# Rows stored in parts, loads split between stores, weights one item later: a change to an attention and convolution kernel

## The chip, the cores and the metric

The kernel runs on one core of a Trainium2 chip. The time is in microseconds of device time for one execution. A core has five engines that run their own instruction lists beside each other: PE (matrix products), DVE (elementwise work on vectors), ACT (functions and copies), POOL and SP (here both used only to start transfers; DVE and ACT also do the arithmetic that PE does not). Transfers are carried by the core's 16 DMA engines. SP and ACT start them by hardware queues, POOL by a software queue.

## The reference

Two images of 256 channels and 64 × 64 points pass through two layers. In plain code, with all that only reshapes left out:

```python
# layer 0
q, k, v = heads(Wq x + bq) / sqrt(32), heads(Wk x + bk), heads(Wv x + bv)   # 8 heads, 4096 points
fuse = softmax(q k^T) v
h = Wf [x, fuse] + bf
x = h * m + x * (1 - m)                        # m: the mask, resized to 64 x 64
# layer 1
x = x * sigmoid(relu(x ca_w1 + ca_b1) ca_w2 + ca_b2)       # per point, over channels
x = x + (window attention over 8 x 8 windows, 4 heads) out_w + out_b
x = channel shuffle of x in 4 groups
y = relu(bn1(conv 7x7 of x, 64 groups, 4 channels in, 1 out))
y = bn2(conv 7x7 of y, 64 groups, 1 channel in, 4 out)
out = x * sigmoid(y)
```

Everything is in 32-bit floats.

## The kernel before

**Projections (0 to 175 us).** q, k and v are computed for 16 chunks of 512 columns (2 images × 8) and stored to DRAM. v is copied out of PSUM by ACT into a staging tile with tag "v" (L499 to L511) and stored by POOL; the last chunk is copied in two halves, by ACT and by DVE. The staging pool has two places, so a tile waits for the stores of the one two before. Then a flag that DVE computed decides a branch; here the first of two arms runs.

**Attention (175 to 2685 us).** `pipeline` runs over 1024 slots: image b, chunk c of 512 query columns, head group g of 4 heads, key block m of 128 keys. Each slot has 16 score matmuls (L666), four exponentials on ACT (L679), products (L718) and a running sum of the exponentials on DVE (L724). When a chunk is through, `denominators` (L752, tile dn) sums over the keys by matmuls, and DVE divides (f, L785). `at(delay, action)` puts an action off by so many slots: a chunk's `stage(b, c)` begins DN + 8 + late slots after the chunk's last one; late is 5, but 0 for the last two chunks, (1,6) and (1,7). The stage is a generator: `run_stages` takes it one step further at every fourth slot, so that its matmuls (hy: fuse convolution; ca1, ca2: channel attention; qk: projection; sc: window scores; pt, o: transposes and products; op: out-projection) lie between the attention's. It makes u (L861), projects q and k of the windows (`project`), and ends with storing the chunk's rows xo to x_s in DRAM (L1047). The stage of (1,6) spans the last chunk's slots; the stage of (1,7) runs when there are none left.

**Convolutions.** `convolve` is a generator over 26 items. Item k is a set u of 4 of the 64 groups, for one image or for both: k = 0 to 8 are u = 0 to 8 of image 0; k = 9 to 15 are u = 2 to 8 of image 1; k = 16 to 21 are u = 9 to 14 of both images at once ("pairs"); k = 22 to 25 are single again (u = 15 of each image, then u = 1 and u = 0 of image 1). The loop at k does, in this order:

- `conv1(k+1)`: the first convolution on PE. Single items have 56 matmuls (L1177); pairs (`conv1_pairs`, L1144) use two operands that DVE made: dx, differences of neighbouring points (L1116), and both, sums of neighbouring weights (L1121, tile "both", "botha" in the profile). At its end it makes them for item k+2 (`differences(k+2)`).
- `conv2(k)`: the second convolution on PE (L1203), then tanh and a copy on ACT (L1214, L1220) into z. z has four places.
- `gate(k)`: z times x on DVE (L1230).
- loads of rows: SP brings the rows of a later item from x_s (L1095), one transfer for each image, up to item k+6.
- `store(k)`: 12 stores for each image, 3 blocks of rows × 4 (L1257; L1255 where ACT starts them), dealt out to the queues of POOL, SP and, in the last two items, ACT.
- `load_w`: SP brings the weights of one u, 896 KB (L1088), into a tile of tag "e", which has 8 places. While `weights[0] <= 1 + EB` (EB is 8) one set is loaded in every item; the later ones, from w10 on, one in every item from k = EARLY + 4 = 13 (EARLY is 9).

Each engine works through its list in the order of the program. The framework counts SP's and ACT's transfers over 8 counters in turn, so that a transfer waits until the one eight before is done.

```python
                z = conv2(k)
...
                gate(k, z)
...
                store(k, z)
                if weights and (weights[0] <= 1 + EB or k >= EARLY + 4):
                    load_w(weights.popleft())
```

Of the kernel before, what the change touches and what calls it, by code (L numbers as in the profile page):

```python
# [57 lines left out]
def conv_seq_kernel(ctx: ExitStack, tc: tile.TileContext, a, out):  # L58
# [315 lines left out]
    with (  # L374
# [109 lines left out]
        for i, (b, c) in enumerate(chunks):  # L484
# [14 lines left out]
            for copy, ms in evict:  # L499
                v = st0.tile([P, KC, 4, P], F32, tag="v", name=f"vst_{b}_{c}_{ms.start}")  # L500
                copy(  # L501
                    v[:, :, ms].rearrange("p g m d -> p m g d"),
                    sv[:, ms].rearrange("p m (g d) -> p m g d", g=KC),
                )
                for g in range(KC):
                    nc.gpsimd.dma_start(
                        v_s[b, g, c][:, ms.start * P : ms.stop * P],
                        v[:, g, ms].rearrange("p m d -> p (m d)"),
                    )
# [46 lines left out]
    def pipeline(arm, shifted, pools):  # L556
# [232 lines left out]
        def stage(b, c):  # L789
# [71 lines left out]
            nc.vector.scalar_tensor_tensor(u, t, 1.0, x1, ALU.add, ALU.mult)  # L861
# [4 lines left out]
            def project(hc):  # L866
                s = psum2(f"qk{tag}_{hc}")
                for j in range(2):
                    o = (KC * j + hc) * P
                    for kc in range(KC):  # L870
                        by_columns(
                            s[:, j, :],
                            wqkv[:, kc, o : o + P],
                            u[:, kc, :],
                            start=(kc == 0),
                            stop=(kc == KC - 1),
                        )
                return s
# [67 lines left out]
            window_exp(0)  # L946
            project_out(1, s)
# [83 lines left out]
            for oc in range(KC):  # L1031
# [5 lines left out]
                for n, (x0, _, _) in enumerate(BLOCKS):  # L1037

                    r0, r1 = max(WS * c, x0 - 1), min(WS * c + WS, x0 + 31)
                    if r0 >= r1:  # L1040
                        continue
                    for h in range(2):
                        q = 2 * oc + h
                        p = 32 * q + 1 - x0

                        eng = nc.sync if h == 1 and (b, c) == (B - 1, NCHUNK - 1) else nc.gpsimd
                        eng.dma_start(  # L1047
                            x_s[b, n, p + r0 : p + r1].rearrange("r g w -> g r w"),
                            xo[64 * h : 64 * h + 64, oc, r0 - WS * c : r1 - WS * c, :],
                        )  # L1050

# [6 lines left out]
        def convolve():  # L1061
# [29 lines left out]
            def load_x(k):  # L1091
                u, images = items[k]
                x = xs[k] = early[k % 4] if k < EARLY else xcs[(k - EARLY) % len(xcs)]
                for i, b in enumerate(images):
                    nc.sync.dma_start(  # L1095
                        x[:, nb * i : nb * i + nb].rearrange("p n g w -> p n (g w)"),
                        x_s[b, :, :, UG * u : UG * u + UG, :].rearrange("n p g w -> p n (g w)"),
                    )

            def load_rows(k):  # L1100

                while len(xs) < min(k + 1, len(items)) and (
                    staged or B - 1 not in items[len(xs)][1]
                ):
                    load_x(len(xs))
# [60 lines left out]
            def conv1(k):  # L1166
# [7 lines left out]
                s = psum1(f"c1{arm}{k}")  # L1174
# [16 lines left out]
                differences(k + 1)  # L1191

            def conv2(k):
# [17 lines left out]
                for m in range(len(images)):  # L1211
# [8 lines left out]
                    nc.scalar.activation(z, z, AF.Copy, bias=0.25, scale=0.25)  # L1220
                    zs.append(z.rearrange("p j (n x) -> p j n x", x=W))
# [4 lines left out]
            def gate(k, zs):  # L1226
                u, images = items[k]
                for m in range(len(images)):
                    x = xs[k][:, nb * m : nb * m + nb, :, PAD : PAD + W]
                    nc.vector.tensor_mul(zs[m], zs[m], x.rearrange("p n g x -> p g n x"))  # L1230

            def store(k, zs):
# [4 lines left out]
                elif k == len(items) - 2:  # L1237
                    engines = (nc.scalar, nc.sync, nc.sync)
                elif k == len(items) - 3:
                    engines = (nc.gpsimd, nc.sync, nc.sync)  # L1240
                elif len(images) == 2:
                    engines = (nc.gpsimd, nc.sync)
                stores = 0
                for m, b in enumerate(images):
                    for n, (x0, r0, r1) in enumerate(BLOCKS):
                        for i in range(4):
# [6 lines left out]
                            eng = engines[stores % len(engines)]  # L1253
                            if eng is nc.scalar:
                                held.append(lambda a=args: nc.scalar.dma_start(*a))  # L1255
                            else:
                                eng.dma_start(*args)  # L1257
                if k == len(items) - 1:
# [3 lines left out]
            def more():  # L1262
                if staged and not xcs:

# [7 lines left out]
                    load_rows(EARLY)  # L1272
                return bool(xcs)
# [9 lines left out]
            for k, (u, images) in enumerate(items):  # L1283
                while len(xs) <= k + 1 < len(items):
                    if not more():
                        yield
                conv1(k + 1)
                yield
                more()
                z = conv2(k)  # L1290
                yield
                more()
                gate(k, z)
                if k == 0:
                    first = z
                    continue
                if xcs:
                    load_rows(min(len(xs) + (k >= EARLY - 1), k + len(xcs)))
                elif k + 4 < EARLY:
                    load_rows(k + 4)  # L1300
                if k == 1:
                    store(0, first)
                store(k, z)
                if weights and (weights[0] <= 1 + EB or k >= EARLY + 4):
# [25 lines left out]
        for i, (b, c, g, m) in enumerate(slots):  # L1330
# [16 lines left out]
            if g == KC - 1 and m == NMB - 1:  # L1347
                late = 5 if (b, c) < (B - 1, NCHUNK - 2) else 0
                if (b, c) == (0, 0):
                    late = EB + 5  # L1350
                at(DN + 8 + late, lambda b=b, c=c: stages.append(stage(b, c)))
# [19 lines left out]
        staged.append(True)  # L1371
# [87 lines left out]
```

## Time and profile before

| | us |
|---|---|
| runs | 2892.77, 2894.96, 2895.96 |
| median | 2894.96 |
| the profiled execution | 2891.88 |
| its span in the profile | 2890.0 |
| PE busy | 2860.5 |
| DVE busy | 2452.6 |
| ACT busy | 2459.4 |
| POOL busy | 571.0 |
| last matmul ends | 2878.25 |
| last SP store issued | 2884.8 |
| last ACT store issued | 2886.5 |

The span runs from the first to the last event of the profile; the execution is 1.88 us longer. The granted clock of PE is 0.997 of full speed over the span. A line of the timeline gives start, length, engine, source line, operation, result and operands, how many instructions are merged in it, and in brackets how long the engine had been idle and what released it. A line of the waits view gives the total in us, the number of waits and the longest. Names in the profile carry the arm as a last letter: c1a is the PSUM tile of the first convolution, xla and xea are rows of x, wa is a set of weights, za is z.

### The profile page before, as it was taken

The numbers are of one execution on the slowest core, as the hardware profiler recorded it, in microseconds if no ns is written. First come the engines' busy times: TensorE is split into PE (matmuls) and PEld (weight loads), VectorE is DVE, ScalarE is ACT, GpSimd is POOL, SyncE is SP. The second block draws the span as 40 slices with busy tenths as digits, with TensorE's granted clock in tenths as the row PEclk, the third lists the DMA queues.
The fourth block names the chain that finished last, engine by engine and source line by source line (L and its number), as shares of the span: only waits on it lengthen the run. The fifth ranks groups of instructions, "written<-read, shape, count | busy, mean of one in ns | idle before, by whom it ended". The sixth has DMA issues, their size and how long they took to land.

```text
span 2890.0 us, 85875 instructions
## 1 busy us (share of the span) xinstructions
PE 2860.5 (99%) x37198; PEld 836.0 (29%) x37198; DVE 2452.6 (85%) x1370; ACT 2459.4 (85%) x4151; POOL 571.0 (20%) x939
## 2 busy tenths in 40 slices
PE   9999999999999999999999999999999999999998
PEld 4541122222222222222222222222222222222676
DVE  3349999999999999999999999999999999999323
ACT  5569989898989898998989898989989898989434
POOL 8111111111111212121120111111211110010376
PEclk9999999999999999999999999999999999999999
DMA  8545433333243434343333334333434432142575
GB/s 262 206 162 189 148 88 74 97 80 91 69 102 77 106 76 95 87 99 87 81 92 75 92 71 96 80 91 84 100 83 89 95 81 84 56 123 64 159 203 137
DMA packets 245755, 305.67 MB, mean 106 GB/s; under 512 B 121272, under 2 KB 137836, under 8 KB 245112
## 3 DMA queue, kind: packets, MB, share of 16 engines
q1 hardware_dynamic: 200084, 231.51, 27.7%
q0 software_dynamic: 40496, 65.79, 12.1%
q8 instruction: 294, 4.82, 0.7%
q10 hardware_dynamic: 4788, 2.79, 0.3%
q14 instruction: 93, 0.76, 0.1%
HBM read 221.88 MB, written 66.39 MB: 100 GB/s over the span
## 4 chain that ended last, share of the span: by engine, by line
PE 94%; DMA 2%; issue 1%; DVE 1%; ACT 1%; SPq 1%; POOL 0%; DVEq 0%; POOLq 0%; ACTq 0%
PE sa L666 36%; PE ava L718 34%; PE hya L552 4%; PE qka L552 4%; PE c2a L1203 2%; PE q L450 2%; PE vwa L552 2%; PE opa L552 2%; PE k L450 2%; PE v L489 2%; PE c1a L1177 1%; PE sca L905 1%; PE c1a L1144 1%; PE oa L999 1%; PE pta L980 1%
## 5 line engine op out<-in xcount | busy, mean ns | idle before, releaser
L679 ACT ACTIVATE ea<-sa 128x512 f32<-128x512 f32 (+1 forms) x3072 | 2038.8, 745 | 56.4 <-PE sa L666 24.3
L666 PE MATMUL sa<-qa,ka 32*64 32x512 f32 x16384 | 1145.7, 614 | 3.0 <-DVE vst L501 2.9
L724 DVE TENSOR_TENSOR suma<-suma,ea 128x2048 f32<-128x2048 f32 x480 | 1096.4, 2284 | 6.2 <-ACT ea L679 1.1
L718 PE MATMUL ava<-ea,va 128*32 128x512 f32 x8192 | 1092.0, 605 | 0.4
L724 DVE TENSOR_TENSOR odda<-odda,ea 128x2048 f32<-128x2048 f32 x420 | 958.3, 2282 | 2.4 <-ACT ea L679 0.5
L696 POOL DMA_DIRECT2D folda<-suma x336 | 235.5, 874 | 1618.4 <-DVE suma L726 1510.3
L666 PEld LDWEIGHTS sa<-qa,ka 32*64 32x64 f32 x16384 | 241.4, 130 | 787.3 <-ACT ea L679 716.7
L718 PEld LDWEIGHTS ava<-ea,va 128*32 128x32 f32 x8192 | 161.6, 108 | 834.0 <-issue 805.2
L1257 POOL DMA_DIRECT2D out_dram<-za x212 | 119.7, 573 | 46.1 <-DVE za L1230 25.6
L552 PE MATMUL qka<-ua,qkv_w 128*32 128x512 f32 x1024 | 115.8, 592 | 0.7 <-DVE ua L861 0.7
L1047 POOL DMA_DIRECT2D xs<-xo x94 | 67.2, 722 | 206.5 <-DVE xo L1032 203.0
L808 ACT ACTIVATE ta<-hya,bf 128x512 f32<-128x512 f32 x32 | 20.2, 684 | 95.2 <-PE hya L552 95.2
L724 DVE TENSOR_TENSOR odda<-ea,ea 128x2048 f32<-128x2048 f32 x30 | 68.6, 2288 | 37.3 <-ACT ea L679 37.3
L469 DVE TENSOR_REDUCE top<-sq 128x128 f32<-128x2048 f32 x16 | 36.6, 2286 | 74.5 <-ACT sq L463 74.5
L764 POOL DMA_DIRECT2D invs<-inva x62 | 34.1, 557 | 287.4 <-DVE inva L779 286.4
L1203 PE MATMUL c2a<-yca,wa 32*64 32x192 f32 (+1 forms) x2912 | 85.0, 368 | 2.2 <-issue 2.0
L926 ACT ACTIVATE ewa<-ewa,mxwa 128x64 f32<-128x64 f32 x256 | 85.3, 346 | 1.5 <-DVE mxwa L917 1.5
L724 DVE TENSOR_TENSOR suma<-ea,ea 128x2048 f32<-128x2048 f32 x32 | 73.2, 2287 | 11.5 <-DMA ka<-ks 8.5
L1214 ACT ACTIVATE za<-c2a 128x384 f32<-128x384 f32 x64 | 27.9, 487 | 62.1 <-PE c2a L1203 34.0
L917 DVE TENSOR_REDUCE mxwa<-ewa 128x8 f32<-128x512 f32 x32 | 21.9, 685 | 63.3 <-ACT ewa L913 63.3
L1203 PEld LDWEIGHTS c2a<-yca,wa 32*64 32x64 f32 x2912 | 67.7, 191 | 18.0 <-issue 10.5
L884 ACT ACTIVATE qka<-qka,qkv_b 128x512 f32<-128x512 f32 x64 | 40.2, 680 | 37.9 <-PE qka L552 37.9
(166 smaller groups left out, 1698.6 us busy)
## 6 DMA issues: line engine op xcount, KB each, us to landing
ka<-ks SPq DMA_DIRECT2D x256, 256.0 KB
va<-vs SPq DMA_DIRECT2D x256, 256.0 KB
wa<-ws SPq DMA_DIRECT2D x17, 896.0 KB
ws<-zeros SPq DMA_DIRECT2D x16, 896.0 KB
folda<-suma POOLq DMA_DIRECT2D x224, 64.0 KB, 3.2
folda<-suma POOLq DMA_DIRECT2D x112, 128.0 KB, 3.6
xs<-xo POOLq DMA_DIRECT2D x78, 140.0 KB, 6.1
qs<-qst SPq DMA_DIRECT2D x16, 512.0 KB
```

What stands on the lines that cost most here:

```text
L450: nc.tensor.matmul(s[:, g, :], w[:, kc, g * P : (g + 1) * P], rhs, start=(kc == 0), stop=(kc == KC - 1),)
L489: nc.tensor.matmul(sv[:, m, :], xs0[i][:, kc, m * P : (m + 1) * P], wv[:, kc, :], start=(kc == 0), stop=(kc == KC - 1),)
L552: nc.tensor.matmul(out[o : o + 32], weights[:, o : o + 32], x, start=start, stop=stop)
L666: nc.tensor.matmul(heads[j][o], k[r, cols][:, o], q[r, g, :], start=True, stop=not shifted)
L679: nc.scalar.activation(e[:, h, :], tile, AF.Exp, scale=SCALE0)
L696: nc.gpsimd.dma_start(dst[p : p + rows], total[rows * k : rows * k + rows, h, :], accum_op=ALU.add if k else ALU.bypass,)
L718: nc.tensor.matmul(av[r, :], v[:, m % PB, r], e[:, j, :], start=start, stop=stop)
L724: nc.vector.tensor_add(total, first.pop(m % chains, total), e)
L926: nc.scalar.activation(e[:, n, :], e[:, n, :], AF.Exp, bias=mx[:, n : n + 1], accum_out=rs[:, n : n + 1],)
L1047: eng.dma_start(x_s[b, n, p + r0 : p + r1].rearrange("r g w -> g r w"), xo[64 * h : 64 * h + 64, oc, r0 - WS * c : r1 - WS * c, :],)
L1203: nc.tensor.matmul(tiles[j // 2][o, j % 2, 0 : n * W], w[r, d, o], y[r, 0:n, d : d + W], start=(d == 0), stop=(d == KS - 1),)
L1257: eng.dma_start(*args)
```

## The change

It has these parts:

1. The staging tile of v has three places instead of two.
2. u is made in two instructions, by channel half, and `project` runs over the channel half outside and q/k inside.
3. In the last chunk's stage the second half of the projection is put out before the first window's exponential.
4. The last chunk's rows are stored in three parts by channel: 12 of 64 channels first, then 44, then 8. Right behind the first part on SP, `last_rows` loads the rows of items 9 to 11.
5. Rows are loaded up to item k+4 always. For single items the load is split by block, into 3 or 6 transfers, and these are put between SP's stores.
6. Single items with odd k use another PSUM bank for the first convolution.
7. The last two items' copy on ACT and gate on DVE are done in three parts, by block.
8. Item 24's stores go to SP, ACT, SP, POOL in turn (6, 3, 3 of 12) instead of 8 on SP and 4 on ACT; those of items 22 and 23 go half to SP and half to POOL.
9. The weights from w10 on are loaded from k = EARLY + 5 = 14, one item later than before.
10. The stage of chunk (1,6) begins 4 slots later.

```diff
@@ -497,7 +497,7 @@
             for copy, ms in evict:
-                v = st0.tile([P, KC, 4, P], F32, tag="v", name=f"vst_{b}_{c}_{ms.start}")
+                v = st0.tile([P, KC, 4, P], F32, tag="v", name=f"vst_{b}_{c}_{ms.start}", bufs=3)
                 copy(
@@ -858,16 +858,19 @@
             u = wp.tile([P, KC, CH], F32, tag="u", name=f"u{tag}")
-            nc.vector.scalar_tensor_tensor(u, t, 1.0, x1, ALU.add, ALU.mult)
+            for oc in range(KC):
+                nc.vector.scalar_tensor_tensor(
+                    u[:, oc], t[:, oc], 1.0, x1[:, oc], ALU.add, ALU.mult
+                )
             yield True
...
                 s = psum2(f"qk{tag}_{hc}")
-                for j in range(2):
-                    o = (KC * j + hc) * P
-                    for kc in range(KC):
+                for kc in range(KC):
+                    for j in range(2):
+                        o = (KC * j + hc) * P
                         by_columns(
@@ -943,8 +946,9 @@
             s = project(1)
-            window_exp(0)
-            project_out(1, s)
+            steps = [lambda: window_exp(0), lambda: project_out(1, s)]
+            for step in steps[::-1] if (b, c) == (B - 1, NCHUNK - 1) else steps:
+                step()
             yield True
@@ -1034,24 +1038,24 @@
                 )
-                for n, (x0, _, _) in enumerate(BLOCKS):
-                    r0, r1 = max(WS * c, x0 - 1), min(WS * c + WS, x0 + 31)
-                    if r0 >= r1:
-                        continue
-                    for h in range(2):
-                        q = 2 * oc + h
-                        p = 32 * q + 1 - x0
-                        eng = nc.sync if h == 1 and (b, c) == (B - 1, NCHUNK - 1) else nc.gpsimd
-                        eng.dma_start(
-                            x_s[b, n, p + r0 : p + r1].rearrange("r g w -> g r w"),
-                            xo[64 * h : 64 * h + 64, oc, r0 - WS * c : r1 - WS * c, :],
-                        )
+            last = (b, c) == (B - 1, NCHUNK - 1)
+            parts = [(UG * 2, UG * 5), (UG * 5, NG), (0, UG * 2)] if last else [(0, NG)]
+            for g0, g1 in parts:
+                for oc in range(KC):
+                    for n, (x0, _, _) in enumerate(BLOCKS):
+                        r0, r1 = max(WS * c, x0 - 1), min(WS * c + WS, x0 + 31)
+                        if r0 >= r1:
+                            continue
+                        for h in range(2):
+                            q = 2 * oc + h
+                            p = 32 * q + 1 - x0
+                            eng = nc.sync if h == 1 and last else nc.gpsimd
+                            eng.dma_start(
+                                x_s[b, n, p + r0 : p + r1, g0:g1].rearrange("r g w -> g r w"),
+                                xo[64 * h + g0 : 64 * h + g1, oc, r0 - WS * c : r1 - WS * c, :],
+                            )
+                if last and g0 == UG * 2:
+                    staged[0](EARLY + 2)
         items = [(u, (0,)) for u in range(EARLY)] + [(u, (1,)) for u in range(2, EARLY)]
@@ -1088,21 +1092,23 @@
                 ws[u] = t
-            def load_x(k):
+            def load_x(k, queue=None):
                 u, images = items[k]
...
                 for i, b in enumerate(images):
-                    nc.sync.dma_start(
-                        x[:, nb * i : nb * i + nb].rearrange("p n g w -> p n (g w)"),
-                        x_s[b, :, :, UG * u : UG * u + UG, :].rearrange("n p g w -> p n (g w)"),
-                    )
-            def load_rows(k):
+                    to = x[:, nb * i : nb * i + nb].rearrange("p n g w -> p n (g w)")
+                    src = x_s[b, :, :, UG * u : UG * u + UG, :].rearrange("n p g w -> p n (g w)")
+                    if queue is None:
+                        nc.sync.dma_start(to, src)
+                    else:
+                        queue.extend((to[:, n], src[:, n]) for n in range(nb))
+            def load_rows(k, queue=None):
                 while len(xs) < min(k + 1, len(items)) and (
-                    staged or B - 1 not in items[len(xs)][1]
+                    xcs or B - 1 not in items[len(xs)][1]
                 ):
-                    load_x(len(xs))
+                    load_x(len(xs), queue)
             halves = {}
@@ -1171,7 +1177,10 @@
                 w = ws[u][:, 0 : 32 * UW].rearrange("p (m g d) -> p g d m", g=UG, d=KS)
-                s = psum1(f"c1{arm}{k}")
+                if k % 2:
+                    s = avp.tile([P, CH], F32, tag="av", name=f"c1{arm}{k}")
+                else:
+                    s = psum1(f"c1{arm}{k}")
                 for d in range(KS):
@@ -1189,6 +1198,11 @@
                 differences(k + 1)
+            def blocks_of(k, t):
+                if k < len(items) - 2:
+                    return [t]
+                return [t[:, :, n] for n in range(nb)]
             def conv2(k):
@@ -1217,8 +1231,10 @@
                         )
-                    nc.scalar.activation(z, z, AF.Copy, bias=0.25, scale=0.25)
-                    zs.append(z.rearrange("p j (n x) -> p j n x", x=W))
+                    z = z.rearrange("p j (n x) -> p j n x", x=W)
+                    for part in blocks_of(k, z):
+                        nc.scalar.activation(part, part, AF.Copy, bias=0.25, scale=0.25)
+                    zs.append(z)
                 while held:
@@ -1227,19 +1243,20 @@
                     x = xs[k][:, nb * m : nb * m + nb, :, PAD : PAD + W]
-                    nc.vector.tensor_mul(zs[m], zs[m], x.rearrange("p n g x -> p g n x"))
-            def store(k, zs):
+                    x = x.rearrange("p n g x -> p g n x")
+                    for z_, x_ in zip(blocks_of(k, zs[m]), blocks_of(k, x)):
+                        nc.vector.tensor_mul(z_, z_, x_)
+            def store(k, zs, queue):
                 u, images = items[k]
...
                 elif k == len(items) - 2:
-                    engines = (nc.scalar, nc.sync, nc.sync)
-                elif k == len(items) - 3:
-                    engines = (nc.gpsimd, nc.sync, nc.sync)
-                elif len(images) == 2:
+                    engines = (nc.sync, nc.scalar, nc.sync, nc.gpsimd)
+                elif k >= len(items) - 4 or len(images) == 2:
                     engines = (nc.gpsimd, nc.sync)
+                each = -(-3 * len(queue) // (nb * 4))
                 stores = 0
@@ -1251,17 +1268,21 @@
                             eng = engines[stores % len(engines)]
+                            for _ in range(each if eng is nc.sync else 0):
+                                if queue:
+                                    nc.sync.dma_start(*queue.popleft())
                             if eng is nc.scalar:
...
                                 eng.dma_start(*args)
+                while queue:
+                    nc.sync.dma_start(*queue.popleft())
                 if k == len(items) - 1:
...
                         held.popleft()()
-            def more():
-                if staged and not xcs:
+            def last_rows(k):
+                if not xcs:
                     for n in range(3):
@@ -1269,8 +1290,9 @@
                         xcs.append(room[:, n : n + 2].rearrange("p k n g w -> p (k n) g w"))
-                    load_rows(EARLY)
-                return bool(xcs)
+                load_rows(k)
+            staged.append(last_rows)
             load_rows(3)
@@ -1282,26 +1304,27 @@
                 while len(xs) <= k + 1 < len(items):
-                    if not more():
+                    if not xcs:
                         yield
+                    else:
+                        load_rows(len(xs))
                 conv1(k + 1)
                 yield
-                more()
                 z = conv2(k)
                 yield
-                more()
                 gate(k, z)
...
                     continue
+                queue = deque()
                 if xcs:
-                    load_rows(min(len(xs) + (k >= EARLY - 1), k + len(xcs)))
+                    load_rows(k + 4, queue if len(images) == 1 else None)
                 elif k + 4 < EARLY:
-                    load_rows(k + 4)
+                    load_rows(k + 4, queue)
                 if k == 1:
-                    store(0, first)
-                store(k, z)
-                if weights and (weights[0] <= 1 + EB or k >= EARLY + 4):
+                    store(0, first, deque())
+                store(k, z, queue)
+                if weights and (weights[0] <= 1 + EB or k >= EARLY + 5):
                     load_w(weights.popleft())
@@ -1348,6 +1371,8 @@
                     late = EB + 5
+                elif (b, c) == (B - 1, NCHUNK - 2):
+                    late = 4
                 at(DN + 8 + late, lambda b=b, c=c: stages.append(stage(b, c)))
@@ -1368,7 +1393,6 @@
                 next(conv)
-        staged.append(True)
         for _ in conv:
```

## The prediction

> **What bounds the kernel now.** I read four views in this order: the page's busy rows, the waits of PE, the timelines around each place that the edits touch, and the order in which the built kernels put their instructions on each engine.
>
> ```profile
> PE 2860.5 (99%) x37198; PEld 836.0 (29%) x37198; DVE 2452.6 (85%) x1370; ACT 2459.4 (85%) x4151; POOL 571.0 (20%) x939
> PE 94%; DMA 2%; issue 1%; DVE 1%; ACT 1%; SPq 1%; POOL 0%; DVEq 0%; POOLq 0%; ACTq 0%
> ```
>
> PE is busy 2860.5 of 2890.0 us, and no edit takes a matmul away. So only PE's gaps and the tail behind its last matmul can be won: 29.5 us in all. The waits of PE that the edits touch, before 2560 us (first line) and after it:
>
> ```profile
> PE sa L666 <- DVE vst L501: 2.9, 1, 2.9
> ...
> PE c1a L1177 <- DMA xla<-xs: 2.7, 1, 2.7
> ...
> PE hya L552 <- DVE fa L785: 0.8, 1, 0.8
> PE qka L552 <- DVE ua L861: 0.7, 1, 0.7
> ```
>
> The columns are us in total, times, longest. The reader should see how little a perfect edit can give; the edit of the weights can open gaps where there are none.
>
> **1. Three places for v.** The last half of v goes out by DVE, which waits for the stores of the tile two back:
>
> ```profile
> 174.88 0.58 ACT L501 COPY vst<-v 128x512 f32<-128x512 f32 x1 [2.44 <-PE v L489]
> 176.67 0.69 DVE L501 COPY vst<-v 128x512 f32<-128x512 f32 x1 [32.86 <-DMA vs<-vst]
> 177.72 5.76 PE L666 MATMUL sa<-qa,ka 32*64 32x512 f32 x48 [2.92 <-DVE vst L501]
> ```
>
> With a third place DVE can start with ACT's half, at about 174.9, 1.8 us earlier; the scores, which take over the PSUM bank, follow. The row allows 1.9. The Trainium skill (Runtime: NRT & Kernel Launch, "Instruction fetch mechanics") speaks against that: a taken branch to a page outside the prefetched window stalls the engine until it is fetched. The branch into the attention lies behind PE's last v matmul (174.80), under this very wait. No row shows PE's fetch alone. By the rule nothing of the 1.9 need be left; SP, whose branch goes the same way, issues its first load (137.48) 1.08 us after the flag's last DVE instruction ended (136.40). If PE needs that too, it is ready near 175.9, still only at the time that the bank is free. I take −1.9, ends −2.9 and 0.
>
> **2. The stage of chunk (1,6) one group later.** DVE, not PE, sets the end of attention: it adds without pause from 2563 to 2684 us, the last 15 in 35.83 us (2.39 each), and the matmul of the sums (dna, at 2685.96, not waiting) needs the last of them. The later stage takes the .75 wait for fa at 2563.5 off PE's path, and two banks for the first convolutions the .59 wait of c1(1) for its bank at 2683.6, but both lie before dna, so PE only reaches dna earlier and waits for DVE. Also the 32 opa matmuls of that stage (3.46 us) move from before the last slots to behind dna: they no longer cover DVE's lag. PE reaches dna 0.75 + 3.46 + 0.59 = 4.8 earlier, of which .9 is covered by the half of dna whose sums exist, and DVE ends about 2 us earlier, as it has less to catch up; I get a wait of about 1.95, and once opa is paid behind dna the last stage starts **+0.6** late. Ends −1.3 (both waits simply go) and +2.
>
> **3. u in two halves, the projection by kc outside, and the out-projection before the exponential.** The first half of u is ready .54 earlier (1.23 whole against .69 a half), so its .7 goes; the scores' .45 wait for ACT's qk goes as the out-projection fills it. **−1.15**; ends −1.15 and 0.3 for one DVE instruction more.
>
> **4. Last rows in parts.** The last chunk's stores (SP 2747.99 to 2750.54) are followed by loads that need them landed, and c1 waits for the load:
>
> ```profile
> 2747.99 2.55 SPq L1047 DMA_DIRECT2D xs<-xo  x2
> ...
> 2755.55 0.93 SPq L1095 DMA_DIRECT2D xla<-xs  x2
> ...
> 2759.30 2.54 PE L1177 MATMUL c1a<-xla,wa 128*32 128x192 f32 x56 [2.69 <-DMA xla<-xs]
> ```
>
> 12 of 64 channels go first now, in stores of 26 KB instead of 140. Stores of 24 KB issued on POOL land in 3.7 us (median, the DMA view after 2740 us), the 140 KB ones in 5.5: landed at about 2751.7, loads out at 2752, 3.6 us for a load (2755.55 to c1's start at 2759.30), so there at 2755.6, before PE is ready (2759.30 − 2.69 = 2756.6). Behind the loads stand four SP stores of the other channels, needed only items later. **−2.5**; ends −2.7 and −1.
>
> **5. Loads of rows by block between the stores, look-ahead k+4.** Single items' loads become 3 or 6 DMAs of a third the size, at .38 us each of SP. SP has room there (12 stores in 8 us at a .38 us issue), and rows are needed four items (20 us or more) later. Only load(4), the third of whose blocks stands behind store(1)'s gate, comes near its use at 2710.3. **0**; ends −1 and +2.
>
> **6. Weights one item later.** This edit decides. A pair's second operand is made by DVE (botha, L1121) from the weights, and DVE has it before the gate of the item two back; SP loads the next weights only after that gate's stores. In the kernel before it barely holds:
>
> ```profile
> 2826.69 0.35 SPq L1088 DMA_DIRECT2D wa<-ws  x1
> 2827.34 0.39 SPq L1095 DMA_DIRECT2D xla<-xs  x1
> 2827.83 8.65 SPq L1257 DMA_DIRECT2D out_dram<-za  x12
> 2836.57 0.35 SPq L1088 DMA_DIRECT2D wa<-ws  x1
> ```
> ```profile
> 2831.86 0.57 DVE L1121 TENSOR_TENSOR botha<-wa 128x384 f32<-128x384 f32 x1 [0.60 <-DMA wa<-ws]
> ...
> 2841.29 0.59 DVE L1121 TENSOR_TENSOR botha<-wa 128x384 f32<-128x384 f32 x1 [1.02 <-DMA wa<-ws]
> ```
> ```profile
> 2833.43 1.38 PE L1144 MATMUL c1a<-xea,botha 128*32 128x192 f32 x24
> ...
> 2842.42 1.35 PE L1144 MATMUL c1a<-xla,botha 128*32 128x192 f32 x24
> ```
>
> Weights issued at 2826.69 land at 2831.8 (5.1 us), botha is done at 2832.43, PE uses it at 2833.43: one microsecond of slack; the next has .54. From there each load moves behind the stores of one item more. The built order shows on SP: store(14), weights 10; on DVE: botha, then the gate of k, then its stores. So a closed loop arises: weights → botha → gate → 12 stores on SP → next weights. One turn: 4.7 (load, the shorter of the two rows) + .58 + .96 (a gate) + 5.6 (12 stores) + .1 = 11.95 us, while PE has 8.97 us of work for a pair (4.1 + 4.87). The 12 stores are the part without a clean row: 7.0 to 9.9 in the trace, there with loads in flight and gates waited for; .38 each at the issue alone (4.6). I take .47 each.
>
> In the time of the kernel before: weights 10 at 2803.3 (where 11 stood, 2802.89, with more blocks before it), landed 2808.0, botha 2808.6: c1(17), at 2804.87, starts 3.75 late. c1(18) +.7 (store(15) is a single item's: 10 DMAs). Weights 12 leave at 2826.0 behind the stores of the gate at 2819.9, so c1(19) +4.05. c1(20) and c1(21) 3.05 each (11.95 − 8.97 and a little), c1(22), which needs no botha, 2.45. Sum 17.05, less 1.7 of PE's own gaps near 2801 to 2807 (.34, .23, 1.09) that fall under the first stall: **+15.4**. The weights for item 24 have an item to spare.
>
> The skill's fit for one transfer (DMA: Bandwidth & Descriptors, "Anatomy of one DMA — SWDGE (gpsimd) path": about 2.0 us + bytes over 436 GB/s) makes 896 KB 4.1 us, for a software queue; the rows of this hardware queue say 4.7 to 5.1. By the rule each of six stalls is .6 shorter, 11.8; I keep the row. Ends: rule and 4.6 us of stores, a turn of 10.35, +7.6; the row of 7.0 us for the stores, a turn of 13.4, +21.5.
>
> **7. The end: queues and parts.** The last c2 ends at 2878.25, the copy at 2879.8, the gate at 2880.8; SP still empties a backlog:
>
> ```profile
> 2856.28 28.48 SPq L1257 DMA_DIRECT2D out_dram<-za  x50
> ```
>
> 50 stores become fewer for items 24, and the last gates go by block, the first out 1.2 us earlier (.84 + .96 become thirds). SP ends at 2884.8, ACT's stores at 2886.5, the span at 2890.0. ACT has 9 instead of 10. Against a larger gain stands that all queues end in the same engines: .57 per store on SP is more than its .38 issue. **−1.8**; ends −2.5 and 0.
>
> **Sum.** −1.9 + 0.6 − 1.15 − 2.5 + 15.4 − 1.8 = +8.65. The span of 2890.0 becomes 2898.7, the profiled execution 2891.9 becomes 2900.5. The median of the runs shown is 2894.96, 3.1 above the profiled one; the sum on the median gives **2903.6**.
>
> **Rivals.**
> (a) The loop turns faster: load 4.1 and stores 4.6 leave +7.6 against −6.75 of gains: +0.9, 2895.8, no change. For it: stores with no weights in flight were not seen alone. Against: a measured load never took under 4.7.
> (b) The other side, faster: the loop does not close. It decides at load + 12 stores = 7.3 us (8.97 − .58 − .96 − .1): below that PE never waits for botha beyond the first shift, and if the earlier rows' loads, fewer now, free SP so that weights 10 leaves by 2799.5 too, the gains stand: −6.75, **2888.2**. Against: it asks for two thirds of the shortest load plus the shortest issue in the trace.
> (c) The loop turns slower, 13.4: +14.8, 2909.7; stores of SP at 7.0 us and more speak for it, that these rows hold other loads against it.
> (d) Attention's edits do nothing and PE's fetch takes v's 1.9: +10.5 to +12, 2905 to 2907; within the forecast's range.
>
> **Numbers.** Chances: forecast with (d) .52, (c) .21, (a) .17, (b) .10. What a measurement here can tell from no change is 0.2%, 5.8 us: 2889.2 to 2900.8. The slower cases give .73, (a) .17, (b) .10. The range, 2893 to 2912, holds the forecast, (a) and nearly all of (c), and leaves out (b) and the tail of (c). The forecast's own range is 2899 to 2908.
>
> **What will show it.** For part 6: PE waiting for botha at five or six c1 after 2800 us, 3 us each, DVE waiting 3 or more for the weights, SP's weights 12 us apart. No such wait, and the forecast is wrong by its largest term. For part 1: scores begin below 176. For part 2: dna waits about 2 us for its sums. For part 4: no wait of c1 for xla near 2756. For part 7: less than 11.75 us between the last c2 and the end.

## The result, and the profile after

| | before | changed |
|---|---|---|
| median of 6 runs, us | 2895.28 | 2906.51 |
| lowest, highest | 2892.66, 2896.23 | 2904.0, 2914.85 |
| ratio, 95% interval | | 1.0046, 1.0033 to 1.0059 |
| span of the profiled execution | 2890.0 | 2903.3 |
| last convolution ends | 2878.25 | 2892.14 |

The changed kernel is slower by 13 us by the ratio (the interval: 10 to 17) and by 11 us by the medians. The forecast was +8.65 and 2903.6; the measured time lies in the stated range, between the forecast and the rival of the slower loop (2909.7). Measured again on another chip (after_again, below) the loss was 15 us.

The page of the changed kernel: the work of PE is the same (2860.5 before), its share of the chain falls from 94% to 91%, and POOL, DMA and "issue" have what PE lost.

```profile
PE 2861.6 (99%) x37198; PEld 838.7 (29%) x37198; DVE 2453.7 (85%) x1390; ACT 2460.6 (85%) x4155; POOL 574.9 (20%) x946
...
PE 91%; DMA 3%; POOL 2%; issue 2%; DVE 1%; SPq 1%; ACT 1%; ACTq 0%; DVEq 0%; POOLq 0%
```

The waits of PE after 2560 us in the changed kernel (us in total, times, longest):

```profile
PE c1a L1150 <- ACT za L1228: 6.3, 3, 3.3
PE c1a L1150 <- DVE botha L1127: 6.1, 2, 5.1
PE c1a L1150 <- issue: 4.5, 1, 4.5
PE dna L752 <- DVE suma L724: 1.8, 1, 1.8
PE c1a L1186 <- DMA wa<-ws: 1.5, 2, 1.0
```

The waits for xla, fa, ua and yca are gone (in the profile of after_again 0.4 us for xla are left). In their place stand 17 us at the first convolution of the pairs (c1a, now L1150). Three releasers are named, but it is one cause. The timelines of DVE and PE around item 19 show it:

```profile
2827.05 0.56 DVE L1127 TENSOR_TENSOR botha<-wa 128x384 f32<-128x384 f32 x1 [6.47 <-DMA wa<-ws]
2827.54 1.83 DVE L1248 TENSOR_TENSOR za<-za,xla 128x768 f32<-128x768 f32 x2
```
```profile
2818.29 4.87 PE L1217 MATMUL c2a<-yca,wa 32*64 32x384 f32 x112
2827.71 2.16 PE L1150 MATMUL c1a<-xea,botha 128*32 128x192 f32 x24 [4.55 <-issue]
```

botha is ready at 2827.61, and PE begins at 2827.71. DVE itself had waited 6.47 us for the weights, and the gates, which stood behind botha in its list, follow at once. So "issue" in PE's bracket is botha too, and so is "ACT za" at items 18, 20 and 21 (botha ends at 2814.01, 2840.62 and 2852.99, c1 begins at 2814.11, 2840.72 and 2853.09): such a wait has to be looked up on the engine that makes the operand, not by the name in the bracket alone. SP closes the loop, in the same stretch of the changed kernel:

```profile
2821.94 0.35 SPq L1092 DMA_DIRECT2D wa<-ws  x1
2822.34 2.36 SPq L1102 DMA_DIRECT2D xla<-xs  x2
2828.53 5.48 SPq L1277 DMA_DIRECT2D out_dram<-za  x12
2834.11 0.35 SPq L1092 DMA_DIRECT2D wa<-ws  x1
```

Weights at 2821.94, botha at 2827.05, gate at 2827.54, stores from 2828.53, next weights at 2834.11: a turn of 12.2 us. The seven loads from w10 on leave at 2797.08 to 2872.66, 12.6 us apart in the mean (9.77 before). From c1 of item 16 to c1 of item 22 PE takes 73.63 us (2790.46 to 2864.09), 54.37 before: +19.3. Up to item 16 the change had won 6.5 us (2796.98 became 2790.46; 4.1 us in the profile of after_again).

The ring has a second branch. In every second turn the gate waits, behind botha, for ACT's copy of z as well. ACT's copy needs the second convolution, and that one stands on PE behind the first convolution that waited for the botha before:

```profile
2813.45 0.56 DVE L1127 TENSOR_TENSOR botha<-wa 128x384 f32<-128x384 f32 x1 [3.20 <-DMA wa<-ws]
2814.62 0.96 DVE L1248 TENSOR_TENSOR za<-za,xla 128x768 f32<-128x768 f32 x1 [0.61 <-ACT za L1236]
```

In these turns PE's own work is part of the ring: it adds 0.61 and 0.33 us here, 1.39 and 1.67 in the profile of after_again.

The last chunk's rows and the end, in the changed kernel:

```profile
2744.55 1.75 SPq L1053 DMA_DIRECT2D xs<-xo  x2
...
2747.90 1.59 SPq L1102 DMA_DIRECT2D xla<-xs  x3
...
2752.87 2.55 PE L1186 MATMUL c1a<-xla,wa 128*32 128x192 f32 x56
```
```profile
2874.24 22.66 SPq L1277 DMA_DIRECT2D out_dram<-za  x36
```

No bracket stands behind PE's row: the rows are there. SP's backlog at the end has 36 stores instead of 50, but ends 4.8 us behind the last convolution instead of 6.5, and the span 11.2 instead of 11.75: little came of it.

### The profile page after: what moved, and what is told of

It is laid out like the page before. It is cut to its first block, busy times and chain, and to the rows that moved or that the text cites. A ratio compares the mean times of both kernels' runs of the same rounds, so it can differ in the third digit from the quotient of the medians.

```text
span 2903.3 us, 85949 instructions
## 1 busy us (share of the span) xinstructions
PE 2861.6 (99%) x37198; PEld 838.7 (29%) x37198; DVE 2453.7 (85%) x1390; ACT 2460.6 (85%) x4155; POOL 574.9 (20%) x946
## 4 chain that ended last, share of the span: by engine, by line
PE 91%; DMA 3%; POOL 2%; issue 2%; DVE 1%; SPq 1%; ACT 1%; ACTq 0%; DVEq 0%; POOLq 0%
PE sa L666 36%; PE ava L718 34%; PE qka L552 4%; PE hya L552 4%; PE v L489 2%; PE vwa L552 2%; PE opa L552 2%; POOL out_dram L1277 2%; PE k L450 1%; PE q L450 1%; DMA out_dram<-za 1%; PE sca L908 1%; DVE suma L724 1%; PE pta L984 1%; PE ca2a L843 1%
## 5 line engine op out<-in xcount | busy, mean ns | idle before, releaser
L808 ACT ACTIVATE ta<-hya,bf 128x512 f32<-128x512 f32 x32 | 20.3, 684 | 94.5 <-PE hya L552 94.5
L1228 ACT ACTIVATE za<-c2a 128x384 f32<-128x384 f32 x64 | 27.9, 487 | 61.8 <-PE c2a L1217 39.0
L920 DVE TENSOR_REDUCE mxwa<-ewa 128x8 f32<-128x512 f32 x32 | 21.9, 685 | 61.0 <-ACT ewa L916 61.0
```

## The experiments

In each table a ratio is to the kernel before on the same chip. The three groups ran on different chips, whose medians of the kernel before were 2898.60, 2895.26 and 2892.90; so ratios are compared, not times.

### First group: is it the weights?

Weights from item 13 again, all else of the change kept (w4):

```diff
-                if weights and (weights[0] <= 1 + EB or k >= EARLY + 5):
+                if weights and (weights[0] <= 1 + EB or k >= EARLY + 4):
```

> The changed kernel with its weights loaded from item 13 again, as before; all else of the change stays. Theory A (the loop weights, botha, gate, 12 stores, next weights makes the whole loss): PE's waits at c1 of items 17 to 22 and 24 go (19.2 and 0.8 us in the changed kernel's trace), span 2883.5, time 19 to 21 us below the changed kernel, so 2885 to 2888, 7 to 10 below the kernel before. Rival B (the later look-ahead of rows and the loads in pieces load SP too, so that the weights stay late): at most half of it goes, 2894 to 2900, and SP's weights still leave 11 us or more apart.

The kernel before with that line changed the other way, EARLY + 4 to EARLY + 5 (before_w5):

> The kernel before with its weights from item 14 on, nothing else changed. Theory A: the loop closes here too, its turn (12.2 us, 5.4 for the load, 0.6, 1.0, 5.3 for the stores) against 9.0 of PE work: 15 to 21 us slower than the kernel before, 2910 to 2916. Rival B (only with the rows' look-ahead of the change does it cost): less than 6 us.

The changed kernel with fewer of a pair's stores on SP (w5_third):

```diff
-                elif k >= len(items) - 4 or len(images) == 2:
+                elif k >= len(items) - 4:
                     engines = (nc.gpsimd, nc.sync)
```

> The changed kernel, but of a pair's 24 stores SP starts 8 instead of 12 and POOL 16. Theory A: four stores of 0.45 us less in each turn, 10.4 instead of 12.2, so 1.5 to 1.9 us less for each of five or six turns: 8 to 11 us below the changed kernel, 2895 to 2898. Rival C (the loads' landing or the memory's traffic sets the turn, not what stands ahead of them on SP): the same traffic, no gain, within 2 us of the changed kernel.

More matmuls ahead of c1 (w5_warm; their result is overwritten, so nothing of the computation is left out):

```diff
+                if k > EARLY + 7:
+                    for n_ in range(44):
+                        nc.tensor.matmul(
+                            mid[0:32], ident[:, 0:32], xs[k][:, 0:n, n_ % 4, 0 : W - 1 : 2],
+                            start=True, stop=True,
+                        )
                 for out_, weights_, x, d, start, stop in terms:
```

> The changed kernel with 44 more matmuls on PE (about 2.5 us, their result is overwritten) ahead of the first convolution of items 17 to 21, so that PE does not pause for over 2.6 us. Theory A (the loop over SP and DVE sets the time, PE's slower clock after a pause, 5.2 us over c1 of 17, 19 and 21, is hidden under the next wait): no change, within 1.5 us of the changed kernel, with granted clock 1.0 in these c1. Rival D (the slower clock is part of the loss): 4 to 5 us below the changed kernel. If the extra matmuls cost, up to 12 us above it.

| | median us | ratio, interval |
|---|---|---|
| w4 | 2893.80 | 0.9989, 0.9979 to 0.9999 |
| before_w5 | 2922.49 | 1.0088, 1.0072 to 1.0103 |
| w5_third | 2911.53 | 1.0052, 1.0036 to 1.0068 |
| w5_warm | 2966.66 | 1.0241, 1.0225 to 1.0257 |

**w4 and before_w5** make one number carry the whole change of sign: with everything else of the change the kernel is a little faster than before, and that number alone makes the kernel before 24 to 25 us slower. In w4's trace the loads leave 7.5 to 11.5 us apart, and from item 16 to the end of the last convolution PE takes 81.3 us, as before (81.3; 101.7 in the changed kernel). Two sizes were missed. w4 won 3 us over before, not 7 to 10; where the rest went is shown below, by parts. And before_w5 lost more than 21 (24 by the medians, 25 by the ratio): its turns are 13.4 us, and its pauses at c1 of items 17 to 22 come to 21.9 us (16.5 in the changed kernel). One term of that is in SP's list: a row load, which waits for the gate as well since its look-ahead of six items takes the gated item's place, stands ahead of the stores; the rest is not settled.

**w5_third** did not bear out its number. Its turns are shorter (11.7 in the mean), with 8 stores in 3.4 to 4.8 us:

```profile
2834.84 3.37 SPq L1277 DMA_DIRECT2D out_dram<-za  x8
2838.61 1.24 SPq L1092 DMA_DIRECT2D wa<-ws  x1
```

From c1 of item 17 to c1 of item 22 it takes 58.6 us, 61.8 and 64.2 in the two profiles of the changed kernel, so inside the loop 3 to 6 us of the 8 to 11 expected are there. In two turns the gate waited 1.05 and 1.97 us behind botha for ACT's copy (the second is named DMA in its bracket, but the copy ended at 2857.69 and the gate began at 2857.72), so PE's branch of the ring kept them long. The rest was lost outside: the first load landed only after 6.6 us and not 4.6, and at the end POOL had a backlog: 14.8 us from the last convolution to the end, 11.2 in the changed kernel. So neither theory is decided by its whole time.

**w5_warm** went far past the pauses: an added matmul (two instructions, all on one strip of 32 columns, all into the same output) takes 0.35 us there and not the 0.057 of the estimate, so that 77 us of them were added. A smaller number of them follows below.

### Second group: the clock, the loads in pieces, the stage

The changed kernel as it is (after_again), for comparison:

> The changed kernel as it is, to stand beside the others on one chip. All theories: 11 to 15 us above the kernel before, a turn of the loop of 12 to 13 us.

w4 with loads of rows whole (w4_whole):

```diff
-                    load_rows(k + 4, queue if len(images) == 1 else None)
+                    load_rows(k + 4)
                 elif k + 4 < EARLY:
-                    load_rows(k + 4, queue)
+                    load_rows(k + 4)
```

> The changed kernel with its weights from item 13, and with each load of rows as one transfer for each image again, ahead of the stores; the look-ahead stays four items. Theory E (the loads in pieces, twice as many transfers of 0.4 us between the stores, keep SP behind, so that botha of items 16 and 17 is late by 1.5 and 2.1 us): these two waits go, 2 to 4 us below the run with the weights from item 13 alone. Rival F (the look-ahead of four items, not the pieces, makes the rows of item 16 late, and weights 10 stand behind four stores in any case): the waits stay, no change within 1 us.

The changed kernel with `range(7)` for `range(44)` in the added matmuls (w5_warm2):

> The changed kernel with 7 more matmuls on PE ahead of the first convolution of items 17 to 21, 0.35 us each by the earlier run, 2.5 us in all for each item; their result is overwritten. Theory A (the loop over SP and DVE sets the time, and PE's slower clock after a pause is hidden under the next wait): no change, within 1.5 us of the changed kernel, at a granted clock of 1.0 in these c1. Rival D (the slower clock is part of the loss): 4 to 5 us below it.

w4 with the stage of (1,6) where it was (w4_late0):

```diff
-                elif (b, c) == (B - 1, NCHUNK - 2):
-                    late = 4
```

> The changed kernel with its weights from item 13, and with the stage of chunk (1,6) where it was before (4 slots earlier). Theory S (DVE's sums end attention, so that the later stage only moves PE's wait to the denominators and puts the out-projection behind them): 0.5 to 2 us below the run with the weights from item 13 alone, no wait at dna, a wait of about 0.8 at hya. Rival G (the later stage takes a wait off PE's path and the rest is hidden): 0.7 to 1.3 us above it.

| | median us | ratio, interval |
|---|---|---|
| after_again | 2909.87 | 1.0055, 1.0038 to 1.0072 |
| w4_whole | 2888.73 | 0.9983, 0.9975 to 0.9991 |
| w5_warm2 | 2913.24 | 1.0064, 1.0039 to 1.0088 |
| w4_late0 | 2887.69 | 0.9974, 0.9967 to 0.9982 |

**The clock.** In the changed kernel PE's clock falls after a pause. The windows view of the changed kernel over the first convolutions of items 17 to 21 shows it (the stretch, its length, busy time and instructions of PE, PEld, DVE, ACT and POOL, the granted clock, the DMA share, GB/s):

```profile
2802.30:2807.90 5.60, 5.56 (x88) 4.09 (x88) 1.16 (x2) 0.32 (x1) 4.50 (x8) 0.70 0.48 117
2814.10:2818.30 4.20, 4.19 (x91) 3.88 (x91) 2.27 (x3) 2.41 (x5) 2.43 (x5) 1.00 0.21 47
2827.70:2834.10 6.40, 6.39 (x88) 4.35 (x88) 2.02 (x3) 0.32 (x1) 5.30 (x10) 0.58 0.53 127
2840.70:2844.90 4.20, 4.17 (x90) 3.89 (x90) 2.27 (x3) 2.05 (x5) 2.70 (x5) 1.00 0.24 45
2853.10:2858.70 5.60, 5.60 (x88) 5.15 (x88) 2.03 (x3) 0.40 (x2) 4.50 (x8) 0.70 0.34 63
```

After pauses of 5.10, 4.55 and 3.33 us the clock is 0.70, 0.58 and 0.70 and c1 takes 5.6 to 6.4 us instead of 4.2; after 1.31 and 1.70 it is 1.00. The Trainium skill (TensorE: Matmul & The Clock Gate, "What's actually happening") says that an idle window of about 3.4 us brings the array to half its clock. These five rows fit it roughly, with a longest harmless pause of 1.70 us and a shortest harmful one of 3.33. Other runs do not: c1 of item 17 ran at 0.70 after a pause of 1.94 us in w5_ahead, but at 1.00 after 2.08 us in w4, and c1 of item 21 at 0.70 after 2.63 us in before_w5. So here the length of the last pause alone does not decide it.

The slower c1 come to 5.2 us. How much of them counts shows first in the gates: only where a gate waited for ACT behind botha was the slow c1 on the ring's path, at most 0.94 us in the changed kernel's profile and 3.06 in that of after_again, up to c1 of item 22. The added matmuls of w5_warm2 are the second test. In its windows view, c1 of item 19:

```profile
2834.40:2838.60 4.20, 4.16 (x88) 3.80 (x88) 2.11 (x3) 0.32 (x1) 3.02 (x6) 1.00 0.49 130
```

Four of the five c1 run at full clock there, and nothing is gained: from item 16 to item 22 it takes 74.8 us, 73.6 and 75.6 in the two profiles of the changed kernel. One reservation: at item 18 botha was ready 2.4 us before PE was through with the added matmuls, which delayed PE's branch of the ring, so a gain of up to that size is not excluded; one of 4 to 5 is not seen. Both tests together: most of the 5.2 us is hidden, and what counts is about 1 to 3 us.

**The pieces.** In w4_whole the two waits for botha of items 16 and 17 (1.45 and 2.08 us in w4) are gone from the trace, but the time is not lower by the 2 to 4 us expected: 0.9983 against 0.9989 and (third group) 0.9985. In its profile pauses named "issue" of 1.79, 0.62 and 1.95 us stand in c2 and c1 near these items. What they are stays open.

**The stage.** In w4 PE waits 2.83 us at dna for DVE's sums. In w4_late0 it does not, and pays at hya instead:

```profile
2560.42 3.64 PE L552 MATMUL hya<-fa,WfT 128*32 128x512 f32 x32 [0.65 <-DVE fa L785]
```

From the first scores to the start of the last stage PE takes 2514.2, 2514.6 and 2515.8 us in the three profiles with the stage undone, and 2514.7 to 2518.1 (mean 2516.3) in nine with it late. Undoing is the better side by about 1.4 us, with a scatter as large; the ratio, 0.9974 against 0.9985 to 0.9989, leans the same way.

### Third group: what stands ahead, and the rest

The changed kernel with the weights of the later items ahead of the stores (w5_ahead):

```diff
+                if weights and k >= EARLY + 5:
+                    load_w(weights.popleft())
                 store(k, z, queue)
-                if weights and (weights[0] <= 1 + EB or k >= EARLY + 5):
+                if weights and k < EARLY + 5 and weights[0] <= 1 + EB:
                     load_w(weights.popleft())
```

> The changed kernel with the weights still from item 14 on, but loaded ahead of that item's stores on SP instead of behind them. Theory A (what stands ahead of the weights on SP, the gate's 12 stores, closes the loop): the loop opens, no wait of DVE for the weights of over 1.5 us, 14 to 18 us below the changed kernel and 0 to 4 below the kernel before. Rival C (the landing of the loads and the memory's traffic set the turn): the same bytes in the same items, so at least half of the loss stays, 6 or more above the kernel before.

w4 once more (w4_again):

> The changed kernel with its weights from item 13, once more, to stand beside the next two on one chip: 3 to 4 us below the kernel before.

w4_late0 and w4_whole together (w4_late0_whole):

> Weights from item 13, the stage of chunk (1,6) where it was before, and each load of rows whole: the three undone together, all else of the change kept. Theories E and S (pieces cost 1.5 to 3.5 us, the later stage 0.5 to 2): 8 to 10 us below the kernel before. If what the pieces cost was chance in single profiles: 7 below, as with the stage alone.

And that with the last chunk's rows stored in one part (late0_whole_one):

```diff
-            parts = [(UG * 2, UG * 5), (UG * 5, NG), (0, UG * 2)] if last else [(0, NG)]
+            parts = [(0, NG)]
...
-                if last and g0 == UG * 2:
+                if last:
                     staged[0](EARLY + 2)
```

> As the one before, but with the last chunk's rows stored in one part again, the loads of rows right behind. Theory P (the parts by channel bring the landing of the rows forward past PE's need): PE waits 2 to 2.7 us for the rows at c1 of item 9 and the time is 1.5 to 2.7 us above the run with parts. Rival H (the loads go out ahead of the other stores, and not the size of the first part, is what helped): no wait, no change within 0.7.

| | median us | ratio, interval |
|---|---|---|
| w5_ahead | 2889.34 | 0.9988, 0.9982 to 0.9995 |
| w4_again | 2888.34 | 0.9985, 0.9978 to 0.9992 |
| w4_late0_whole | 2884.03 | 0.9975, 0.9963 to 0.9986 |
| late0_whole_one | 2886.86 | 0.9980, 0.9969 to 0.9990 |

**w5_ahead** bears out that it is the place in SP's list that counts. The weights are loaded in the same items and with the same bytes, only ahead of 12 stores, and the whole loss goes (1.0046 and 1.0055 to 0.9988):

```profile
2823.52 0.43 SPq L1092 DMA_DIRECT2D wa<-ws  x1
2824.07 10.03 SPq L1277 DMA_DIRECT2D out_dram<-za  x12
```

It is close to a repetition of w4, though: on SP's list, ahead of one item's stores is behind those of the item before, and only the item's loads of rows stand between them in addition. The expectation was missed in the waits: pauses of 1.43, 1.94, 1.38 and 3.14 us stand at c1 of items 16, 17, 20 and 21, and DVE waits 1.6, 2.9 and 5.0 us for weights, so the loop is open but without slack.

**w4_late0_whole** and w4_late0 are the fastest kernels of the study, both 7 us under the kernel before by the ratio (0.9975 and 0.9974), and not to be told from each other. That is what was expected if the pieces cost nothing in time; the 8 to 10 us of the theory that they cost 1.5 to 3.5 did not come. **late0_whole_one** shows the worth of the parts. Its timeline, and PE's wait:

```profile
2742.32 2.24 SPq L1053 DMA_DIRECT2D xs<-xo  x2
...
2749.98 1.46 SPq L1102 DMA_DIRECT2D xla<-xs  x3
2754.48 2.79 PE L1186 MATMUL c1a<-xla,wa 128*32 128x192 f32 x32 [3.37 <-DMA xla<-xs]
```

The loads go out 7.7 us behind the first store, 3.2 in w4_late0_whole (3.4 in the changed kernel, 2744.55 to 2747.90), and PE waits 3.37 us, 0.19 with parts. The time is higher by 2.8 us by the medians and by 1.4 by the ratios, in intervals that overlap: the wait is shown, its worth in time only likely.

## Why the prediction was right

**Part 6, the weights** (+15.4, measured +19.3 from item 16 to 22 in one profile; between the changed kernel and w4 from item 16 to the last convolution 20.3, 101.7 against 81.3): right in mechanism, in place and nearly in the waits. PE's pauses at c1 of items 17 to 22 are 5.10, 1.31, 4.55, 1.70, 3.33 and 0.48, together 16.5, forecast 17.05. Mis-sized is the turn: 11.95 forecast, 12.6 and 13.0 in the two profiles. Of its terms the 12 stores, the one called uncertain, held: 5.64 in the mean of five, forecast 5.6. The load of the weights, taken at the shorter row of 4.7, took 4.60 to 5.94 until botha began, 5.26 in the mean of five. The skill's 4.1, which was weighed against the row, would have been further off. Two things were not foreseen. The gate waits for ACT's copy in every second turn (0.94 and 3.06 us in all in the two profiles), so the sum of the turn lacked PE's branch. And the slower clock after a pause makes c1 5.2 us longer; together with the pauses of 16.5, less the 1.7 of PE's own gaps, that makes 20.0, against 19.3 measured. So the pauses came near the forecast, and the loss was larger. That the weights of item 24 "have an item to spare" was wrong: c1 of item 24 waits 1.05 us for them.

**Part 1, v** (−1.9, measured −1.17: the wait is 1.75 instead of 2.92 in every profile with three places). The step "DVE can start with ACT's half" failed. The end of the projections, in the changed kernel:

```profile
175.67 0.58 ACT L501 COPY vst<-v 128x512 f32<-128x512 f32 x1 [2.44 <-PE v L489]
176.29 0.69 DVE L501 COPY vst<-v 128x512 f32<-128x512 f32 x1 [31.69 <-ACT vst L501]
177.34 2.97 PE L666 MATMUL sa<-qa,ka 32*64 32x512 f32 x32 [1.75 <-DVE vst L501]
```

DVE begins .04 after ACT ends: it waits for ACT's copy too, which the stores had hidden. The fetch that the skill's rule on branches spoke for could cost nothing beyond this wait.

**Part 2, the stage** (+0.6): PE waits for DVE at dna as said, 1.75 and 2.36 (forecast 1.95). Against the kernel before (2517.7 us from the first scores to the last stage, 2517.1 in before_w5) the sum was pessimistic by about 1.7: late stages begin 1.1 earlier in the mean.

**Parts 3 and 4** (−1.15, −2.5): the waits for ua, for qk and for the rows are gone. A new pause of .65 ("issue") stands at pta.

**Part 5, the loads** (0, ends −1 and +2): not free in the trace. botha of item 16 comes 1.03 and 1.28 us late in the changed kernel, where it did not wait before.

**Part 7, the end** (−1.8): failed, for the most part. From the last convolution to the end it is 11.2 and 11.0 us in the changed kernel, 11.85 and 12.1 in w4 and w4_again, 11.75 before. ACT's first store leaves 0.8 us behind the last convolution instead of 2.3 (1.1 in w4, 1.6 in w4_again). The gates in parts are not the reason: the first three of ACT's nine stores are item 24's, kept back until the last copies. Why the first leaves earlier is not shown. The eight stores behind it take 0.75 us each. The span ends 3.5 to 3.7 us behind ACT's last store in the kernel before, the changed one, w4 and w4_again alike, which speaks for this row setting the end:

```profile
2893.62 6.02 ACTq L1275 DMA_DIRECT2D out_dram<-za  x8
```

Before it was 5.94 us for ten. SP's shorter backlog ended 2.7 us ahead of this row (2896.90 against 2899.64).

With the weights repaired the gains of the other parts come to 3 to 5 us (w4, w4_again), not the 6.75 of the sum: the end gave nothing, v 0.7 less, and PE's waits for botha took 3.5 us in w4 and 2.4 in w4_again, with 1.3 more for rows. Parts 1, 3 and 7 were not run alone; what is said of them is read from the profiles.

**The sum.** The number came nearer than its terms. Between the spans of the two profiles 13.3 us stand: 6.5 won up to c1 of item 16 (forecast 4.95), 19.3 lost from there to c1 of item 22 (15.4), 1.15 lost from there to the end of the last convolution (0), 0.6 won behind it (1.8). That the first miss works against the other three was luck; the sign, the place and the shape of the loss were not. One count was loose: rival (b) asks for 2.7 of the 4.7 us of the shortest load (7.3 less the 4.6 of the stores' shortest issue), somewhat over half of it and not two thirds.

## What to carry to other kernels

A load that stands behind stores in one queue's list is only as early as what those stores wait for. Before moving it by one item, follow the ring: who uses what it brings, what stands behind that user on its engine, and whether this is what the stores wait for. If so, the sum of the ring, by its longest branch, and no longer the busiest engine, is the period, and a slack of 0.5 to 1 us before says nothing of the 20 us behind it.

A wait that hides a second one is worth only the difference of the two; the instruction's other waits, not only the named releaser, are to be read before it is priced.

## What was not expected of the hardware

- PE's granted clock fell to 0.58 to 0.70 over the matmuls that followed pauses of 3.3 us and more in the changed kernel, and stayed at 1.00 after 1.7 us and less; between these, pauses of 1.94 and 2.63 us (w5_ahead, before_w5) brought it to 0.70, and one of 2.08 (w4) did not. It cost 1.4 to 2.3 us at each such c1 of the changed kernel, but only about 1 to 3 us in all in the time, since for the most part another branch of the loop set the period.
- The same 896 KB load took 4.60 to 5.94 us from its issue to its use in one execution of the changed kernel.
- An instruction of the matmuls on one strip of 32 columns took 0.177 us (87 in 15.41 us, w5_warm); the convolutions, which go round the four strips, took 0.056 (24 in 1.35 us). The former also wrote the same output each time; which of the two makes the difference was not tested.
